# Layer 0's experts on one core: weight transfers are made to wait for the first slots, and six key projections go between the expert pairs

## The chip, the cores and the metric

The kernel runs on one core of one Trainium2 chip. The metric is the device time in microseconds. The kernel before was run three times: 2267.32, 2272.30 and 2272.84 us, a median of 2272.3 us. A separate execution was profiled; every row of a profile shown here is from that one execution. All times in rows are microseconds from the start of its span, unless a column says otherwise.

## What is computed

Four layers, each of them a cross attention followed by a mixture of experts, on 1024 tokens of width 256 (2 batches of 512) and a context of 2048 rows (2 batches of 1024). The change lies in layer 0's experts. Their reference, cut to what matters:

```python
logits = x @ router_w + router_b
route = softmax(logits, axis=1)
max_prob, max_ind = route.max(1), route.argmax(1)
for e in range(8):                       # experts, F = 1024
    h = x @ w1[e]                        # 256 -> 2048
    a, g = split(h, 2)
    y = silu(a) * g @ w2[e]              # 1024 -> 256
    out = where(max_ind == e, y, out)
out = out * max_prob
```

Layer 1's attention, which follows, needs keys and values of the normed context, `ctx @ Wkv`, for each of the two batches. They depend on nothing that layer 0's experts compute, so the kernel projects them early, during those experts.

## The kernel before

**Slots.** Each token's row is scattered to a place ("slot") in a DRAM buffer `xd`, sorted by expert, by eight indirect DMAs on GpSimd (L429; `si` holds the places). An expert has a front of 64 slots; what does not fit goes into overflow tiles of 128 slots, all of one expert. Slots come back as tiles `xs` of 128 rows, loaded by SyncE (L446). Each of these loads depends on all eight scatters.

**Tiles.** `pair_tile(s)` (four of them, s = 0 to 3) works on the fronts of experts 2s and 2s+1 at once: one `xs` tile, two weight tiles `w` loaded by SyncE at L465. `slot_tile(4 + s)` works on an overflow tile; its expert is known only at run time, so its weights are gathered by an indirect DMA on GpSimd (L524). Every weight tile has 3072 KB. The program order is pair 0, overflow tile 4, pair 1, tile 5, pair 2, tile 6, pair 3, tile 7, then tiles 8 and 9, and further tiles in a branch taken only if they are in use.

**Weight buffers.** The pool `L0g` has four buffers, handed out in turn: pair 0 takes buffers 0 and 1, tile 4 buffer 2, pair 1 buffers 3 and 0, tile 5 buffer 1, pair 2 buffers 2 and 3, tile 6 buffer 0, pair 3 buffers 1 and 2, and so on. Thus three of SyncE's transfers (both of pair 0, the first of pair 1) and tile 4's gather can start before any tile is computed; pair 1's second has to wait until pair 0 is done with buffer 0.

**Projections.** `ahead1(…, b)` makes the keys and values of layer 1 for batch `b` in 16 jobs: 8 of keys, then 8 of values. A job is two matmuls of 128x128 by 128x512 (four records in the trace, since each f32 matmul shows two) into a PSUM tile whose tag alternates between "a" and "g" (two buffers each, shared with the experts), a copy on ScalarE (L629 for keys, L649 for values) into `sk` (two buffers), and a 256 KB write to DRAM, issued by ScalarE (L633 to `kd`, L650 to `vd`). Batch 0 is done by `first_batch`, the `filler`, between the scatters and the first pair; batch 1 after the last tile. Then `combine` gathers the experts' results back, eight indirect DMAs on GpSimd (L609), and layer 1 starts with a layer norm of X.

**Order.** The order on each engine is set by the tile framework from the program order and its own priorities; each engine then runs its list strictly in order. A DMA signals its end on one of eight counters for SyncE and ScalarE together, handed out in turn, and a DMA that takes a counter again has a wait on it. GpSimd's DMAs have eight counters of their own.

Of the kernel before, what the change touches and what calls it, by code (L numbers as in the profile page):

```python
# [12 lines left out]
AF = mybir.ActivationFunctionType  # L13
# [4 lines left out]
P = 128  # L18
# [7 lines left out]
E = 8  # L26
# [7 lines left out]
def tile_kernel(ctx: ExitStack, tc: tile.TileContext, d: dict, out: bass.AP):  # L34
    nc = tc.nc
# [370 lines left out]

    FRONT = {"L0": E // 2, "L1": E, "L2": E, "L3": E}

    def moe(L, ps, hp, ep, rows, slots, wrow, used, F, act, glu, finish, filler=None, hold=None):

# [2 lines left out]
        front = FRONT[L]  # L415
        NS = front + wrow.shape[1]
        FT, W1 = F // P, (2 * F if glu else F)
        xd, yd = xds[L]
# [4 lines left out]
        for i, si in enumerate(slots):  # L423
            if named and i == 0:
                nc.vector.tensor_copy(rows[:, :, D], c_tok)
            for t in range(TT):
                if i == 1:
                    nc.vector.tensor_scalar(rows[:, t, D:], c_tok[:, t : t + 1], float(NT), None, ALU.add)
                x = nc.gpsimd.indirect_dma_start(  # L429
                    out=xd, out_offset=bass.IndirectOffsetOnAxis(ap=si[:, t : t + 1], axis=0), in_=rows[:, t, :], in_offset=None  # L430
                ).ins
# [5 lines left out]
        wd = d[f"{L}_experts"]  # L437
        WC = wd.shape[1]

        def parts(w):  # L440
            w1 = w[:, 0 : 2 * W1].rearrange("p (c f) -> p c f", c=2)
            return w1, w[:, 2 * W1 : 2 * W1 + FT * D].rearrange("p (t f) -> p t f", t=FT)

        def turned_slots(s):
            xs = hp.tile([P, RW], F32, tag="xs", name="xs", bufs=4)
            x = nc.sync.dma_start(xs, xd[s * P : (s + 1) * P, :]).ins  # L446
            for y in put:
                tc.add_manual_dep(
                    x, y.name, mybir.DependencyInfo(mybir.DependencyClass.Sync, mybir.DependencyReason.DATA),
                    reason="rows from any scatter",  # L450
                )
            pt = ps.tile([P, 2, P], F32, tag="mm", name="pt")
            for dc in range(2):
                nc.tensor.transpose(pt[:, dc, :], xs[:, dc * P : (dc + 1) * P], ident)
            sT = hp.tile([P, 2, P], F32, tag="sT", name="sT", bufs=3)
            nc.vector.tensor_copy(sT, pt)  # L456
            return xs, sT

        def pair_tile(s):


            ws = []
            for j in range(2):
                w = ep.tile([P, WC], F32, tag="w", name="w")
                nc.sync.dma_start(w, wd[(2 * s + j) * P : (2 * s + j + 1) * P, :])  # L465
                ws.append(parts(w))
            sT = turned_slots(s)[1]
            hT = hp.tile([P, FT, P], F32, tag="hT", name="hT")
            y = ps.tile([P, D], F32, tag="y", name="y")
            hs = {}  # L470

            def half(tag, c0):
                pa = ps.tile([P, 512], F32, tag=tag, name="p" + tag)
                for dc in range(2):
                    for j in range(2):
                        cols = slice(64 * j, 64 * j + 64)
                        nc.tensor.matmul(
                            pa[cols, :], sT[:, dc, cols], ws[j][0][:, dc, c0 : c0 + 512], start=(dc == 0), stop=(dc == 1)
                        )
                return pa  # L480

            def hidden(c, pa, pg):
                a = hp.tile([P, 512], F32, tag="act", name="act")
                nc.scalar.activation(a, pa, act)
                nc.vector.tensor_mul(a, a, pg)
                hs[c] = a

            def turn(c):
                pt = ps.tile([P, 4, P], F32, tag="mm", name="pt")
                for f in range(4):  # L490
                    nc.tensor.transpose(pt[:, f, :], hs[c][:, f * P : (f + 1) * P], ident)
                nc.vector.tensor_copy(hT[:, 4 * c : 4 * c + 4, :], pt)

            def product(c):
                for f in range(4 * c, 4 * c + 4):
                    for j in range(2):
                        cols = slice(64 * j, 64 * j + 64)
                        nc.tensor.matmul(
                            y[cols, :], hT[:, f, cols], ws[j][1][:, f, :], start=(f == 0), stop=(f == FT - 1)
                        )  # L500

            pa = half("a", 0)
            hidden(0, pa, half("g", F))
            pa = half("a", 512)
            turn(0)
            hidden(1, pa, half("g", F + 512))
            product(0)
            turn(1)
            product(1)
            yo = hp.tile([P, D], F32, tag="yo", name="yo", bufs=3)  # L510
            nc.scalar.copy(yo, y)
            nc.scalar.dma_start(yd[s * P : (s + 1) * P, :], yo)

        def slot_tile(s):
            w = ep.tile([P, WC], F32, tag="w", name="w")
            if s < front:
                x = nc.sync.dma_start(w, wd[s * P : (s + 1) * P, :]).ins
                if hold is not None and s < 4:
                    tc.add_manual_dep(
                        x, hold.name, mybir.DependencyInfo(mybir.DependencyClass.Sync, mybir.DependencyReason.DATA),  # L520
                        reason="not among the transfers that the attention waits for",
                    )
            else:
                nc.gpsimd.indirect_dma_start(  # L524
                    out=w, out_offset=None, in_=wd,
                    in_offset=bass.IndirectOffsetOnAxis(ap=wrow[:, s - front : s - front + 1], axis=0),
                )
            w1, w2 = parts(w)
            xs, sT = turned_slots(s)
            hT = hp.tile([P, FT, P], F32, tag="hT", name="hT")  # L530
            for f4 in range(0, FT, 4):
                pa = ps.tile([P, 4, P], F32, tag="a", name="pa")
                for f in range(4):
                    mm2(pa[:, f, :], w1, slice((f4 + f) * P, (f4 + f + 1) * P), sT, slice(0, P))
                to = hT[:, f4 : f4 + 4, :]
                if not glu:
                    nc.scalar.activation(to, pa, act)  # L537
                    continue
                pg = ps.tile([P, 4, P], F32, tag="g", name="pg")
                for f in range(4):  # L540
                    mm2(pg[:, f, :], w1, slice(F + (f4 + f) * P, F + (f4 + f + 1) * P), sT, slice(0, P))
                a = hp.tile([P, 4, P], F32, tag="act", name="act")
                nc.scalar.activation(a, pa, act)
                nc.vector.tensor_mul(to, a, pg)  # L544
            y = ps.tile([P, D], F32, tag="y", name="y")
            for f in range(FT):
                nc.tensor.matmul(y, hT[:, f, :], w2[:, f, :], start=(f == 0), stop=(f == FT - 1))  # L547
            yo = hp.tile([P, D], F32, tag="yo", name="yo", bufs=3)
            finish(yo, y, w)
            if not named:  # L550
                nc.scalar.dma_start(yd[s * P : (s + 1) * P, :], yo)
                return
            to = hp.tile([P, 2], F32, tag="to", name="to", bufs=8)
            nc.vector.tensor_scalar(to[:, 0:1], xs[:, D:], 2.0 * NT, float(s * P), ALU.is_ge, ALU.mult)
            nc.vector.tensor_add(to[:, 1:2], to[:, 0:1], xs[:, D:])
            ti = hp.tile([P, 1], I32, tag="ti", name="ti", bufs=8)
            nc.vector.tensor_copy(ti, to[:, 1:2])
            x = nc.gpsimd.indirect_dma_start(
                out=yd, out_offset=bass.IndirectOffsetOnAxis(ap=ti[:, 0:1], axis=0), in_=yo, in_offset=None
            ).ins  # L560
            for y in out_of:
                tc.declare_no_dep(x, y, reason="rows of different tokens")
            out_of.append(x)

        always = front + ALWAYS[L]
        if front == E:
            for s in range(always):
                slot_tile(s)
        else:
            for s in range(front):  # L570
                pair_tile(s)
                slot_tile(front + s)
            for s in range(2 * front, always):
                slot_tile(s)
# [61 lines left out]

    kds, vds = {}, {}

    def ahead1(ps, st, w, cT, b):

        if b == 0:
            kds["L1"] = dram.tile([B * 4 * P, S], F32, tag="L1kd", name="kd")
# [9 lines left out]
        jobs = []  # L652
# [1 line left out]
            for hf in range(2):  # L654
                jobs.append(("k", (b * 4 + pr) * P, hf * 512, slice(pr * P, (pr + 1) * P), b * S + hf * 512))
        jobs += [("v", kt) for kt in range(8)]
        ahead(ps, st, "L1", w, cT, jobs, values)

    def ahead16(ps, st, L, params, nkt):

# [95 lines left out]
    with (  # L756
# [39 lines left out]
        cT = cp.tile([P, 2, B * S], F32, tag="cT", name="cT")  # L796
        xn = kp.tile([P, TT, D], F32, tag="v", name="xn")
# [219 lines left out]
    with (  # L1017
# [23 lines left out]
            to_T(ps, cT, C, CT, g_c, b_c, "g")  # L1041
            ahead1(ps, hp, wkv, cT, 0)

        yd = moe("L0", ps, hp, ep, xn, slots, wrow, used, 1024, AF.Silu, True, plain, first_batch)
        ahead1(ps, hp, wkv, cT, 1)
        combine(fp.tile([P, TT, D], F32, tag="xn", name="yg"), yd, slots, [mp], X)


# [520 lines left out]
    first = {}  # L1569
# [268 lines left out]
```

## Time and profile before

| what | value |
|---|---|
| median of three runs | 2272.3 us |
| the profiled execution's own time | 2271.54 us |
| its span | 2269.7 us |
| TensorE busy | 2063.8 us, 91% of the span |
| VectorE, ScalarE, GpSimd busy | 1083.0, 859.2, 439.3 us |
| mean DMA rate over the span | 132 GB/s |
| layer 0's experts, first weight issue to first scores of layer 1 | 467.2 to 712.7 |

How to read a row of the timeline: start, duration, engine, line of the kernel, operation, output<-inputs, shape, count of records merged, and in brackets the idle time of the engine just before and what ended it. An engine with a "q" (SPq, ACTq) issues DMAs; the duration is that of issuing, not of the transfer. In a table by stage, each engine has its busy time and, in parentheses, its count of instructions; PEclk is the TensorE clock that was granted, 1.00 being full speed. The releaser in brackets is inferred: where a wait is for several things, the last by the profile is named.

### The profile page before, as it was taken

Reading aid. Unit: us, or ns where it says so; the run is one execution under the profiler, and the core shown is the slowest. Engines: PE = TensorE matmul, PEld = TensorE weight load, DVE = VectorE, ACT = ScalarE, POOL = GpSimd, SP = SyncE. Lnnn points to the kernel's source line nnn. Section 1 sums busy time; section 2 is a strip of 40 time slices with the busy share of each in tenths; the row PEclk is TensorE's granted clock in tenths of the full one; section 3 lists DMA queues with packets and bytes.
Section 4 is the critical chain, followed back from the end, with each engine's and each line's share of the span. In section 5 each row is a group of like instructions: output and inputs, shape, how many; then the busy total and the mean of one; then the engine's idle time right before and its main releaser. Section 6 shows DMA issues by size and latency. Waiting matters only on the chain. (4 is left out here: it accounts for less than half of the span.)

```text
span 2269.7 us, 29982 instructions
## 1 busy us (share of the span) xinstructions
PE 2063.8 (91%) x11532; PEld 1208.1 (53%) x11532; DVE 1083.0 (48%) x2157; ACT 859.2 (38%) x1645; POOL 439.3 (19%) x420
## 2 busy tenths in 40 slices
PE   7999999968898999999898898899699999579996
PEld 3444444444574445544686344589433333479995
DVE  7766666741124655665312884201377773422223
ACT  4444444421114656555112243222135556223333
POOL 2222223210012111210101122312123220111210
PEclk9999999988999999999899998999889999789998
DMA  4222222266835101000554612678410101547771
GB/s 128 70 61 75 70 74 58 88 266 268 332 126 130 47 28 38 28 10 28 179 179 157 230 40 74 219 284 312 138 47 28 32 19 25 249 180 294 312 310 64
DMA packets 111703, 300.72 MB, mean 132 GB/s; under 512 B 23232, under 2 KB 76224, under 8 KB 102848
## 3 DMA queue, kind: packets, MB, share of 16 engines
q1 hardware_dynamic: 76048, 159.30, 20.9%
q0 software_dynamic: 9888, 104.49, 11.9%
q10 hardware_dynamic: 25616, 34.90, 4.2%
q8 instruction: 97, 1.59, 0.3%
q14 instruction: 54, 0.44, 0.1%
HBM read 242.93 MB, written 47.66 MB: 128 GB/s over the span
## 5 line engine op out<-in xcount | busy, mean ns | idle before, releaser
L1432 ACT ACTIVATE p<-s 128x512 f32<-128x512 f32 (+3 forms) x384 | 185.9, 545 | 177.8 <-PE s L1431 116.3
L1374 PE MATMUL s<-kT,qT 32*128 32x512 f32 (+3 forms) x768 | 216.8, 603 | 8.7 <-DVE nm L1380 4.5
L132 PE MATMUL pa<-sT,w 128*128 128x128 f32 x1664 | 205.0, 278 | 8.7 <-DVE sT L456 3.7
L132 PEld LDWEIGHTS pa<-sT,w 128*128 128x128 f32 x1664 | 197.1, 193 | 17.2 <-ACT sq L1613 5.8
L547 PE MATMUL y<-w,hT 128*128 128x256 f32 x832 | 192.8, 384 | 9.3 <-ACT hT L537 4.3
L1431 PE MATMUL s<-qA,kT 32*128 32x512 f32 (+3 forms) x768 | 197.5, 592 | 1.3 <-ACT p L1432 0.9
L1384 DVE TENSOR_REDUCE mx<-s 128x1 f32<-128x512 f32 x256 | 163.5, 684 | 54.3 <-PE s L1374 33.6
L547 PEld LDWEIGHTS y<-w,hT 128*128 128x128 f32 x832 | 154.7, 192 | 31.7 <-DVE hT L544 6.1
L1119 ACT ACTIVATE p<-s,nm 128x512 f32<-128x512 f32 x192 | 129.3, 685 | 84.2 <-DVE nm L1116 84.2
L954 ACT ACTIVATE p<-s 128x1024 f32<-128x1024 f32 x128 | 124.1, 1021 | 90.0 <-PE s L949 90.0
L955 DVE TENSOR_SCALAR p<-p 128x1024 f32<-128x1024 f32 x128 | 108.4, 855 | 95.4 <-ACT p L954 95.4
L1116 DVE TENSOR_REDUCE nm<-s 128x2 f32<-128x1024 f32 x96 | 113.2, 1221 | 83.4 <-PE s L1112 83.4
L149 POOL TENSOR_TENSOR kT<-kT,turned 128x512 f32<-128x512 f32 x62 | 100.6, 1628 | 215.3 <-DVE turned L147 209.1
L960 DVE TENSOR_TENSOR acc<-acc,p 128x1024 f32<-128x1024 f32 x96 | 132.5, 1381 | 2.8
L132 PE MATMUL pg<-sT,w 128*128 128x128 f32 x1056 | 129.3, 276 | 0.0
L880 PE MATMUL o<-p,v 128*64 128x512 f32 x512 | 125.0, 606 | 3.8 <-DVE p L955 3.8
L949 PE MATMUL s<-qT,kT 64*128 64x512 f32 x512 | 127.2, 615 | 0.0
L544 DVE TENSOR_TENSOR hT<-act,pg 128x512 f32<-128x512 f32 x66 | 45.0, 687 | 169.7 <-PE pg L132 147.9
L132 PEld LDWEIGHTS pg<-sT,w 128*128 128x128 f32 x1056 | 123.9, 193 | 0.0
L148 POOL TENSOR_TENSOR kT<-kT,cos 128x512 f32<-128x512 f32 x62 | 87.8, 1425 | 134.7 <-DMA turned<-kT 63.4
L1407 PE MATMUL o<-p,v 128*32 128x256 f32 (+3 forms) x1280 | 107.3, 406 | 6.9 <-POOL p L1436 6.7
L1133 PEld LDWEIGHTS pt<-ident,p 128*128 128x128 f32 x768 | 86.4, 142 | 49.7 <-issue 24.5
(295 smaller groups left out, 3039.6 us busy)
## 6 DMA issues: line engine op xcount, KB each, us to landing
w<-in_L_experts_dram SPq DMA_DIRECT2D x8, 3200.0 KB
w<-in_L_experts_dram SPq DMA_DIRECT2D x8, 3072.0 KB
w<-in_L_experts_dram SPq DMA_DIRECT2D x8, 2048.0 KB
w<-in_L_experts_dram SPq DMA_DIRECT2D x8, 1536.0 KB
kd<-sk ACTq DMA_DIRECT2D x40, 256.0 KB
kT<-kd SPq DMA_DIRECT2D x16, 512.0 KB
turned<-kT SPq DMA_DIRECT2D x60, 128.0 KB
v<-vd SPq DMA_DIRECT2D x12, 512.0 KB
```

Source lines behind the costliest of these rows:

```text
L132: nc.tensor.matmul(ps_ap, lhsT[:, dc, lcols], rhs[:, dc, rcols], start=(dc == 0), stop=(dc == 1))
L547: nc.tensor.matmul(y, hT[:, f, :], w2[:, f, :], start=(f == 0), stop=(f == FT - 1))
L880: nc.tensor.matmul(G[n]["o"][64 * j : 64 * j + 64, :], V[g, b][:, kt, pr * P + 64 * j : pr * P + 64 * j + 64], p[:, j, :], start=(kt == 0) ...
L949: nc.tensor.matmul(s1[:, j, :], G[n]["kT"][r, kt * P : (kt + 1) * P], G[n]["qT"][r, :], start=True, stop=True)
L954: G[n]["exp"] = nc.scalar.activation(p, s1, AF.Exp, scale=0.125).ins
L960: nc.vector.tensor_add(G[n]["acc"], G[n]["acc"], p)
L1116: nc.vector.tensor_reduce(nm[:, qt, :, c], s1, AX.X, ALU.max, negate=True)
L1119: nc.scalar.activation(p[:, j, :], s1[:, j, :], AF.Exp, bias=nm[:, qt, j, c : c + 1], accum_out=l[:, qt, j, c : c + 1],)
L1374: nc.tensor.matmul(s1[:, :w], qT[r, qt * P : (qt + 1) * P], kT[r, c * 512 : c * 512 + w], start=True, stop=True)
L1384: nc.vector.tensor_reduce(mx[:, qt, j, c : c + 1], s1, AX.X, ALU.max)
L1431: nc.tensor.matmul(s2[:, qs], kT[r, kt * P : (kt + 1) * P], qA[r, qs], start=True, stop=True)
L1432: nc.scalar.activation(p[:, j, qs], s2[:, qs], AF.Exp, scale=0.25)
```

## The change

It has two parts. First, weight transfers get a dependence on the first `xs` load, so that they are issued only when it has landed: those of pairs 1 to 3 (of which only the first of pair 1 started earlier before) and the gather of overflow tile 4. Second, `ahead1` gets a slice of its job list, and `moe` a hook between the pairs: before pairs 1, 2 and 3 two key jobs each of batch 1 are run, and the other ten jobs stay behind the last tile.

```diff
+        first_slots = []
+        def behind_slots(x):
+            tc.add_manual_dep(x, first_slots[0].name, ...Sync...)
...
         def turned_slots(s):
             x = nc.sync.dma_start(xs, xd[s * P : (s + 1) * P, :]).ins
+            first_slots.append(x)
...
         def pair_tile(s):
-                nc.sync.dma_start(w, wd[(2 * s + j) * P : (2 * s + j + 1) * P, :])
+                x = nc.sync.dma_start(w, wd[(2 * s + j) * P : (2 * s + j + 1) * P, :]).ins
+                if s > 0:
+                    behind_slots(x)
...
         def slot_tile(s):
-                nc.gpsimd.indirect_dma_start(out=w, ...)
+                x = nc.gpsimd.indirect_dma_start(out=w, ...).ins
+                if front < E and s == front:
+                    behind_slots(x)
...
             for s in range(front):
+                between(s)
                 pair_tile(s)
                 slot_tile(front + s)
...
-        ahead(ps, st, "L1", w, cT, jobs, values)
+        ahead(ps, st, "L1", w, cT, jobs[part], values)
...
+        def between(s):
+            if s > 0:
+                ahead1(ps, hp, wkv, cT, 1, slice(2 * s - 2, 2 * s))
...
-        yd = moe("L0", ps, hp, ep, xn, slots, wrow, used, 1024, AF.Silu, True, plain, first_batch)
-        ahead1(ps, hp, wkv, cT, 1)
+        yd = moe("L0", ps, hp, ep, xn, slots, wrow, used, 1024, AF.Silu, True, plain, first_batch, None, between)
+        ahead1(ps, hp, wkv, cT, 1, slice(6, None))
```

As the changed program is built, GpSimd's list has the eight scatters ahead of tile 4's gather, where before the gather stood first. SyncE's list has pair 0's two weights, the context transfer `cTr` (2048 KB, for layer 2), four `xs` loads, and then the first weights of pair 1, which stood third before. ScalarE's and TensorE's lists have the six key jobs between an overflow tile and the next pair; VectorE's list is unchanged. The waits change with the order: the eighth value write of batch 0 (L650) takes the counter of pair 1's first weights and waits for them, and the first `xs` load waits on a counter last used by batch 0's first key write instead of by its seventh.

More of the change, by code (lines that the diff above doesn't have):

```diff
@@ L407, in tile_kernel, with moe @@
     FRONT = {"L0": E // 2, "L1": E, "L2": E, "L3": E}
-    def moe(L, ps, hp, ep, rows, slots, wrow, used, F, act, glu, finish, filler=None, hold=None):
+    def moe(L, ps, hp, ep, rows, slots, wrow, used, F, act, glu, finish, filler=None, hold=None, between=None):
         front = FRONT[L]
@@ L438, in moe @@
         WC = wd.shape[1]
+        first_slots = []
+        def behind_slots(x):
+            tc.add_manual_dep(
+                x, first_slots[0].name, mybir.DependencyInfo(mybir.DependencyClass.Sync, mybir.DependencyReason.DATA),
+                reason="not among the transfers that the first tile waits for",
+            )
         def parts(w):
@@ L523, in slot_tile @@
             else:
-                nc.gpsimd.indirect_dma_start(
+                x = nc.gpsimd.indirect_dma_start(
                     out=w, out_offset=None, in_=wd,
                     in_offset=bass.IndirectOffsetOnAxis(ap=wrow[:, s - front : s - front + 1], axis=0),
-                )
+                ).ins
+                if front < E and s == front:
+                    behind_slots(x)
             w1, w2 = parts(w)
@@ L637, in tile_kernel, with ahead1 @@
     kds, vds = {}, {}
-    def ahead1(ps, st, w, cT, b):
+    def ahead1(ps, st, w, cT, b, part=slice(None)):
         if b == 0:
```

## The prediction

> **What bounds the kernel now.** The page has TensorE busy for 91% of the span, so I looked for places where TensorE stands idle or slow inside the stretch that the change touches (467 to 713 us). The table by stage of that stretch comes first:
>
> ```profile
> 499.00:502.00 3.00, 0.15 (x1) 0.00 (x0) 0.00 (x0) 0.00 (x0) 2.17 (x3) 1.00 0.97 367
> 502.00:505.00 3.00, 0.00 (x0) 0.00 (x0) 0.00 (x0) 0.00 (x0) 0.74 (x1) 0.74 0.87 301
> ...
> 535.00:540.00 5.00, 4.20 (x30) 1.99 (x28) 2.07 (x3) 1.09 (x2) 0.00 (x0) 1.00 0.00 0
> ...
> 556.00:560.00 4.00, 0.68 (x4) 0.22 (x4) 0.00 (x0) 0.00 (x0) 0.00 (x0) 0.76 0.95 404
> 560.00:564.00 4.00, 4.00 (x10) 1.03 (x10) 0.00 (x0) 0.50 (x1) 0.00 (x0) 0.50 1.00 429
> ```
>
> Where TensorE (first column) is idle, the DMA share (last but one) is near 1; at 535 to 540 no byte moves. After an idle stretch the granted clock is 0.50. The timeline says what is moved and who waits:
>
> ```profile
> 467.20 1.28 SPq L465 DMA_DIRECT2D w<-in_L_experts_dram  x3
> 492.59 1.20 POOL L524 DMA_INDIRECT w<-in_L_experts_dram,wrow  x1 [38.40 <-DMA kd<-sk]
> 494.10 1.00 POOL L429 DMA_INDIRECT xd<-xn,si  x1 [0.30 <-issue]
> 506.97 0.97 POOL L429 DMA_INDIRECT xd<-xn,si  x1 [4.23 <-DMA w<-in_L_experts_dram,wrow]
> 507.54 0.58 ACT L629 COPY sk<-pk 128x512 f32<-128x512 f32 x1 [11.10 <-DMA kd<-sk]
> 508.18 6.42 PE L132 MATMUL pk<-wkv,cT 128*128 128x512 f32 x8 [9.02 <-ACT sk L629]
> 517.05 12.26 PE L132 MATMUL pk<-wkv,cT 128*128 128x512 f32 x24 [2.46 <-ACT sk L629]
> 559.79 2.82 PE L477 MATMUL pa<-w,sT 128*64 128x512 f32 x5 [3.33 <-DMA w<-in_L_experts_dram]
> 590.44 1.50 PE L477 MATMUL pa<-w,sT 128*64 128x512 f32 x5 [2.65 <-DMA w<-in_L_experts_dram]
> 618.70 2.07 PE L477 MATMUL pa<-w,sT 128*64 128x512 f32 x5 [2.78 <-SPq L575]
> ```
>
> Four weight tiles are in flight from 467 to 507. Beside them a 256 KB key write takes 10 to 12 us, `sk` has two buffers, so ScalarE's copies wait, then TensorE's projections of batch 0 (9.0 and 2.5 us). The first pair stands behind those projections. Tile 4's gather also goes ahead of all scatters on GpSimd, and the eighth scatter waits for it. Later, each of pairs 1 to 3 waits for its second weight tile. Two more views end the stretch: SyncE's waits from 460 to 560, and the timeline at its end:
>
> ```profile
> SPq L446 <- DMA kd<-sk: 10.8, 2, 10.6
> ...
> 684.00 0.21 ACT L62 ACTIVATE rsq<-rsq 128x8 f32<-128x8 f32 x1 [4.91 <-DVE rsq L61]
> ...
> 698.68 3.28 DVE L98 TENSOR_SCALAR xn<-X,mv,rsq 128x256 f32<-128x256 f32 x8 [12.96 <-PE pk L132]
> ```
>
> The first slot load (issued at 520.62) ended its wait on a key write, which has nothing to do with slots: it had taken that write's completion counter. And layer 1's norm, ready at 685.7, waits for batch 1's last projection at 698.6.
>
> **Part 1: the slots go first.** Scatters: `si` is written by 491.67. Layer 1's experts have this order already: there `si` is written at 1113.50, the first scatter starts at 1113.78 and the slot load is issued at 1125.50, 11.7 us on. So here: scatter at 491.95, slot load at 503.7, landed at 505.6 (1.9 us, a load of layer 3 in the chain of waits), not 522.5. Its counter is now the first key write's, long done.
>
> Pair 0's two tiles alone end the weight traffic near 483 (6.3 MB at the 425 GB/s of 470 to 490). `cTr`, freed by the transposes of C, then follows at about 485 and not 507.5. So the key copies run at TensorE's pace: 24 records took 10.7 us where nothing stopped them, 1.75 us a job, and uncongested copies came two in 3.7 us (520.6 to 531). I put the eighth key copy at 500, value copies at 502, 503, 505.5, 506.6, 508.7.
>
> Then the two waiting transfers start, near 506. Two such tiles issued together took 15.9, 15.2 and 15.4 us before (543.9 to 559.8, 575.2 to 590.4, 603.3 to 618.7), some 400 GB/s; with 1.3 MB of value writes between them I take 17 us: landed at 523. What is caught with them is the fourth and later value writes, at 10 to 12 us each as above: sixth copy at 520, seventh at 522, eighth at 524.2.
>
> [...] The row at 507.54 shows ScalarE held 11.1 us for a write. The eighth value write is bound to pair 1's first weights by the counter, and in ScalarE's list the table load (1.28 us) and pair 0's first silu stand behind it; behind the silu stand VectorE's product, TensorE's transposes and all the rest of pair 0. [...] Before, the silu started at 534.9. **Gain 8.4**, less 0.6 for a cold clock after TensorE's new wait (bounds: none, and the 2.4 us that 5 us of half speed cost at 560): pair 0 ends at 536.0, not 543.8. **Gain 7.8**, bounds 0 and 18.
>
> Tile 4's weights (landed 523) are needed only at 536. The new wait of the gather holds nothing on GpSimd but later gathers; on SyncE the weights stand behind four slot loads whose counters are done, and before them no load is delayed.
>
> **Part 2: six jobs into the gaps.** Two jobs are 3.5 us of TensorE, two copies and two write issues on ScalarE (2 x 0.58 + 2 x 0.33 = 1.8 us, while it has no silu to do), and 0.5 MB of writes. A period from pair end to pair end lasted 31.4, 28.1 and 29.9 us, 89.4 in sum. Its work is an overflow tile of 10.5 us (543.8 to 554.3) and a pair of 15.0 us (528.7 to 543.8), so 25.5; the rest is waiting and cold clock. With the jobs it is 29.0 by TensorE. By DMA: second weights issued at the pair's end, landed 15.4 later, 12.8 us of work after that (590.4 to 603.2) is 28.2. TensorE decides: 3 x 29.0 = 87.1, a **gain of 2.3**. [...] The rows differ: gaps of 3.3 and 2.8 us were followed by matmuls of over 1.0 us for 4 to 5 us, one of 2.65 was not. [...] Contention from the writes: they are issued some 14 us into a load of 15.4, so I cost 0.2, bounds 0 and 1.3 us a period (0.5 MB at 400 GB/s). **Gain 2.1**.
>
> **The tail.** After the last tile (668.0) ten jobs remain. Their copies run to the fifth at 677, then ScalarE waits with the layer norm's square root for VectorE (684.0), which hangs on the gathers and doesn't move: 16.0 us after the branch, as before. Five more copies then took 7.9 us (684.0 to 691.9), so the last value write is issued near 24 us after the branch, not 32.7. The key fetch of layer 1, issued at 701.86 right after the last writes, follows it. Gain 8.1 by this, 11.4 if TensorE's six jobs of 1.9 us (30.6 for 16) counted in full; I take **9.0**, nearer the queue. The norm no longer waits: its projection ends at about 687 before shifts, its own input at 685.7.
>
> Sum: 7.8 + 2.1 + 9.0 = 18.9 from the profiled execution's own 2271.5 us, so 2252.6; the median of the runs is 0.8 above that execution. Forecast **2253**, own range 2245 to 2260. Nothing behind layer 1's start is touched.
>
> **Rivals.** (a) *The front gain is lost*: waiting weights land near 533 rather than 523, the silu is back where it was; 2271.5 - 2.1 - 9 = 2260. For it: the counter. Against it: two tiles in 15 to 16 us, three times. 0.14.
> [...] 0.14.
> (c) *The jobs move but hide nothing*: each gap stays beside its 3.5 us (10.5 lost), front gain 6, tail 9: 2267. For it: the DMA share is 0.95 to 1.00 in the gaps. 0.10.
> (d) *Slower: loads pace the pairs.* Without the early loads, pair 1's and tile 4's transfers, the value writes and then the key writes come bunched, and the rate falls to the 300 GB/s of 502 to 505. Then the first two land at 531, front gain 1, and later second weights take 22.7 us (6.3 + 0.5 MB): 3 x (22.7 + 12.8) = 106.5, 17 lost; 2271.5 + 17.1 - 1 - 9 = 2279. It decides from a load time of 20.5 us on, against 15.2 to 15.9 measured. 0.10.
> The forecast has 0.52.
>
> **The numbers.** No change that a measurement of this kernel can tell is within 0.3%, 6.8 us. Faster: forecast, (a), (b), 0.80. Same: (c), 0.10. Slower: (d), 0.10. The range of 8 in 10 reaches from (b) to just past (a): 2242 to 2264.
>
> **What would show it.** First slot load issued at about 504; tile 4's gather behind the scatters; no wait of TensorE at 499; a write issue of ScalarE at L650 (changed line number) that ends with pair 1's weights, at 521 to 526, and the silu right behind. Pair ends at 536, 565, 594, 623. No 1.0 us matmuls in pairs 1 to 3. Branch at 658, ten copies, square root at 674, first scores of layer 1 near 694. Wrong if the eighth write is issued long before the weights land, if the second weights of a pair take over 20 us, or if the gaps ahead of pairs keep 3 us beside the jobs.

## The result, and the profile after

| kernel | median | runs | lowest to highest | ratio to before, 95% interval |
|---|---|---|---|---|
| before | 2270.9 us | 13 | 2263.8 to 2280.4 | |
| changed | 2259.5 us | 13 | 2253.1 to 2265.2 | 0.9954 [0.9937, 0.9971] |

The change makes the kernel faster by 11.4 us of the medians. The forecast was 18.9 us, so the time lies inside the range, near its upper end, and where rival (a) put it (2260). The profiled execution of the changed kernel took 2264.7 us, with a span of 2262.7 us. The timeline of the changed kernel shows what became of the front:

```profile
468.34 0.80 SPq L475 DMA_DIRECT2D w<-in_L_experts_dram  x2
473.96 6.93 PE L132 MATMUL pl<-rw,xT 128*128 128x8 f32 x32
495.98 1.22 POOL L429 DMA_INDIRECT xd<-xn,si  x1 [43.41 <-DVE si L379]
502.79 13.90 PE L132 MATMUL pk<-wkv,cT 128*128 128x512 f32 x32
508.61 1.84 SPq L455 DMA_DIRECT2D xs<-xd  x4
511.09 0.33 SPq L475 DMA_DIRECT2D w<-in_L_experts_dram  x1
511.09 0.36 ACTq L665 DMA_DIRECT2D vd<-sv  x1
511.98 0.98 POOL L536 DMA_INDIRECT w<-in_L_experts_dram,wrow  x1 [5.92 <-DMA vd<-sv]
512.36 0.33 ACTq L665 DMA_DIRECT2D vd<-sv  x1
...
528.40 0.59 ACT L664 COPY sv<-pk 128x512 f32<-128x512 f32 x1 [16.07 <-DMA vd<-sv]
529.03 3.68 PE L489 MATMUL pa<-w,sT 128*64 128x512 f32 x8 [12.13 <-ACT sv L664]
532.09 0.59 ACT L664 COPY sv<-pk 128x512 f32<-128x512 f32 x1 [3.11 <-DMA vd<-sv]
...
535.40 0.33 ACTq L665 DMA_DIRECT2D vd<-sv  x1
537.11 1.09 ACT L496 ACTIVATE act<-pa 128x512 f32<-128x512 f32 x2
```

The order is the one that was meant: pair 0's weights, scatters, slots, then the two waiting transfers. The waits of 9.0 and 2.5 us in TensorE's projections are gone (the row at 502.79 is one block of 32 records). But a wait of 12.1 us has come up at 529.03, ahead of pair 0's own matmuls. It ends with a value copy, and that copy waited 16.1 us for a value write. The first silu starts at 537.1; before, it started at 534.9.

SyncE's waits from 460 to 560, in the changed kernel, answer to the row that named a key write before (columns: total, times, longest):

```profile
SPq L455 <- DMA xd<-xn,si: 19.2, 3, 18.1
```

The slot load now waits for the scatters, which it needs, and for no key write. The table by stage of the changed kernel (TensorE's busy time first; clock, DMA share and GB/s last):

```profile
516.00:520.00 4.00, 0.91 (x4) 0.28 (x2) 0.42 (x1) 0.00 (x0) 0.00 (x0) 1.00 1.04 443
520.00:524.00 4.00, 0.00 (x0) 0.00 (x0) 0.00 (x0) 0.00 (x0) 0.00 (x0) 0.61 1.00 429
524.00:528.00 4.00, 0.00 (x0) 0.00 (x0) 0.00 (x0) 0.00 (x0) 0.00 (x0) 0.50 1.04 423
528.00:532.00 4.00, 2.96 (x8) 0.77 (x8) 0.00 (x0) 0.59 (x1) 0.00 (x0) 0.50 0.42 161
...
556.00:561.00 5.00, 4.50 (x14) 2.19 (x13) 0.42 (x1) 1.54 (x3) 0.00 (x0) 1.00 1.02 437
561.00:565.00 4.00, 3.94 (x18) 1.29 (x20) 0.00 (x0) 0.60 (x1) 0.00 (x0) 1.00 1.02 437
```

From 520 to 528 no engine is busy at all while the DMA engines run full (share 1.00 and 1.04): everything waits for the waiting transfers to pass. After 528 the rate falls (161 GB/s from 528 to 532); the trace's list of transfers gives the gather 19.1 us from issue to landing, so the last of the two tiles is in near 531. The last two rows are the gap ahead of pair 1, which was idle before and is full now. The same timeline, for pair 1 and for the end of the stretch:

```profile
556.68 3.60 PE L132 MATMUL pk<-cT,wkv 128*128 128x512 f32 x8
561.06 2.34 PE L489 MATMUL pa<-w,sT 128*64 128x512 f32 x7 [0.56 <-ACT sk L644]
...
682.75 0.21 ACT L62 ACTIVATE rsq<-rsq 128x8 f32<-128x8 f32 x1 [4.84 <-DVE rsq L61]
686.88 3.28 DVE L98 TENSOR_SCALAR xn<-X,mv,rsq 128x256 f32<-128x256 f32 x8 [2.40 <-PE pk L132]
700.95 1.99 PE L1132 MATMUL s<-kT,qT 64*128 64x512 f32 x8 [1.74 <-POOL kT L149]
```

Two key jobs stand in the gap, and the wait behind them is 0.6 us where it was 3.3. At the end the norm waits 2.4 us for TensorE, not 13.0.

| part (us of the profiled executions) | before | after | gained | forecast |
|---|---|---|---|---|
| end of pair 0 | 543.8 | 546.0 | -2.2 | 7.8 |
| three periods, pair 0's end to pair 3's end | 89.4 | 85.0 | 4.4 | 2.1 |
| pair 3's end to the branch | 34.8 | 35.1 | -0.2 | 0 |
| branch to the first scores of layer 1 | 44.7 | 34.9 | 9.7 | 9.0 |

These sum to 11.7 us at the first scores of layer 1. The span is only 7.0 us shorter: 4.7 us are lost later in that execution, in stages that the change leaves alone; over the whole execution the mean granted clock was 0.950 against 0.958. The medians give 11.4.

So the second part of the change did what was expected, and more. The question is the first part: why did it gain nothing? Three causes were on the table when the experiments were planned. **A**: value writes of batch 0 are caught beside the two waiting tiles, for longer than I had put. **B**: the counter that the eighth value write shares with pair 1's weights holds ScalarE, as the prediction had it. **C**: the front was only unlucky in its clock. The router's matmuls (`pl`, x32) took 6.9 us in this execution, at a granted clock of 0.50 (473.9 to 480.9), and 3.9 us before, at 0.93 (472.7 to 476.7), and everything behind them is late.

### The profile page after: what moved, and what is told of

It is laid out like the page before. It is cut to its first block, busy times and chain, and to the rows that moved or that the text cites. A ratio compares the mean times of both kernels' runs of the same rounds, so it can differ in the third digit from the quotient of the medians.

```text
span 2262.7 us, 29983 instructions
## 1 busy us (share of the span) xinstructions
PE 2070.5 (92%) x11532; PEld 1218.9 (54%) x11532; DVE 1083.6 (48%) x2157; ACT 859.6 (38%) x1645; POOL 439.3 (19%) x420
```

## The experiments

The kernel before ran again beside each group: 2270.3 us in 19 runs beside the first four, 2273.2 us in 12 runs beside the last four. The ratios are to these, and each edit is shown against the changed kernel.

### Each part of the change alone

The first part alone: the hook between the pairs does nothing, and batch 1's 16 jobs all stay behind the last tile.

```diff
         def between(s):
-            if s > 0:
-                ahead1(ps, hp, wkv, cT, 1, slice(2 * s - 2, 2 * s))
+            return
...
-        ahead1(ps, hp, wkv, cT, 1, slice(6, None))
+        ahead1(ps, hp, wkv, cT, 1)
```

> The first part alone: the waiting weights, with all 16 jobs of batch 1 behind the last tile. Theory A (the value writes of batch 0 are caught beside the two weight tiles that wait, and ScalarE's copies with them): pair 0 ends 76 to 78 us after the first weight issue, as in both profiles (76.6 before, 77.6 changed), pairs 1 to 3 still wait for their second weights, ratio to before 0.998 to 1.003. Theory B (the prediction's sizes, ScalarE held by the eighth value write's counter until pair 1's weights land): pair 0 ends 69 us after the first weight issue and ScalarE's issue of the eighth write ends with those weights, ratio 0.996 to 0.997. Theory C (the front gain is there, and a cold TensorE clock in the router hid it in the one changed profile): pair 0 ends 73 to 74 us after, ratio 0.997 to 0.998.

Measured: 2273.1 us in 14 runs, ratio 1.0006 [0.9992, 1.002]. The second part alone: no transfer waits for the slots.

```diff
         def behind_slots(x):
+            return
```

> The second part alone: the six jobs between the pairs, weights and gather as before. All theories: the three periods sum to 85 to 88 us (89.4 before), the tail is 9 to 10 us shorter. Theory A: with the first part worth nothing, this is all of the change: ratio 0.993 to 0.995, within 3 us of the changed kernel. Theories B and C: the first part adds 4 to 8 us, so this one is slower than the changed kernel by that: ratio 0.997 to 0.9985 by the prediction's sizes.

Measured: 2257.5 us in 6 runs, ratio 0.9945 [0.9925, 0.9965]. The change as a whole has 0.9954 [0.9937, 0.9971]. The second part is all of the gain; the first is worth nothing that can be measured. In the first part's profile pair 0 ends 77.6 us after the first weight issue (76.6 before), as A had it. In the second part's profile the three periods sum to 85.8 us, and the way from the branch to the first scores takes 35.0 us. The timeline of the first part alone has the gaps ahead of the pairs back:

```profile
561.85 2.78 PE L489 MATMUL pa<-w,sT 128*64 128x512 f32 x5 [3.07 <-DMA w<-in_L_experts_dram]
...
591.50 1.73 PE L489 MATMUL pa<-w,sT 128*64 128x512 f32 x5 [2.47 <-DMA w<-in_L_experts_dram]
...
621.61 1.50 PE L489 MATMUL pa<-w,sT 128*64 128x512 f32 x5 [2.93 <-SPq L590]
```

That of the second part alone has one short wait left in their place:

```profile
559.86 1.50 PE L490 MATMUL pa<-w,sT 128*64 128x512 f32 x5 [0.86 <-DMA w<-in_L_experts_dram]
```

So the gaps are closed by the jobs, with or without the waits on the slots.

### The value writes taken out of the way

If A holds, the loss in front goes when no value write meets a waiting tile. There are two ways to get there. In the first, both tiles wait for the last value write of batch 0 rather than for the slots:

```diff
         def behind_slots(x):
             tc.add_manual_dep(
-                x, first_slots[0].name, ...
+                x, value_writes[7].name, ...
...
+    value_writes = []
...
-            nc.scalar.dma_start(vds["L1"][r, :], v)
+            value_writes.append(nc.scalar.dma_start(vds["L1"][r, :], v).ins)
```

> The changed kernel, but the waiting transfers (tile 4's gather, pair 1's first weights) depend on the last value write of batch 0 instead of on the first slots. Theory A: with no weights beside them the value copies run two in 3.7 us, the first silu comes 52 to 56 us after the first weight issue (68.8 in the changed kernel, 67.7 before), pair 0 ends at 62 to 66 us; tile 4 then waits for its weights until about 72, so 4 to 6 us of it remain: 2252 to 2256 us. Theory B: the same front, since the counter is released by the dependence itself, but no gain beyond 3 us. Theory C: no change in the front against the changed kernel.

Measured: 2250.1 us in 6 runs, ratio 0.9903 [0.9879, 0.9928]; by the ratios that is 0.5%, some 11 us, below the changed kernel. In the other, four of batch 0's eight value jobs go behind the last tile, and the waits stay as in the change:

```diff
...
-            ahead1(ps, hp, wkv, cT, 0)
+            ahead1(ps, hp, wkv, cT, 0, slice(0, 12))
...
         ahead1(ps, hp, wkv, cT, 1, slice(6, None))
+        ahead1(ps, hp, wkv, cT, 0, slice(12, None))
```

> The changed kernel, but only the first 4 of batch 0's 8 value jobs stay ahead of pair 0, and the other 4 go behind the last tile. Theory A: no value copy is left to be caught, pair 0 starts as soon as the slots are in, its first silu comes 48 to 52 us after the first weight issue and pair 0 ends near 60; the four jobs cost 7 us in the tail; in sum 2248 to 2253 us. Theory B: nothing stands behind a counter of weights any more, the same. Theory C: the front gains nothing, and the tail's 7 us make it slower than the changed kernel: 2264 to 2268.

Measured: 2247.9 us in 6 runs, ratio 0.9899 [0.9875, 0.9922]. The timeline of the kernel whose tiles wait for the last value write:

```profile
516.94 0.59 ACT L665 COPY sv<-pk 128x512 f32<-128x512 f32 x1 [0.46 <-DMA vd<-sv]
...
520.30 0.60 ACT L496 ACTIVATE act<-pa 128x512 f32<-128x512 f32 x1
...
538.07 3.75 PE L132 MATMUL pa<-sT,w 128*128 128x128 f32 x16 [7.84 <-DMA w<-in_L_experts_dram,wrow]
```

The eighth value copy is at 516.9 (it was at 534.8), the silu at 520.3 (537.1), and pair 0 ends at 529.9 (546.0). Half of that is given back at once: tile 4 now waits 7.8 us for its weights. With four values late pair 0 ends at 519.7, and tile 4 waits 6.0 us:

```profile
510.06 0.60 ACT L496 ACTIVATE act<-pa 128x512 f32<-128x512 f32 x1
...
525.67 3.76 PE L132 MATMUL pa<-sT,w 128*128 128x128 f32 x16 [6.04 <-DMA w<-in_L_experts_dram,wrow]
```

Some 7 us of that front are the four jobs themselves, which are only moved: that kernel takes 42.0 us from the branch to the first scores of layer 1, where the changed kernel takes 34.9. The kernel with the waits on the last value write moves no job, so it is the cleaner of the two.

The kernel whose tiles wait for the last value write had the slow router too (7.0 us), and its pair 0 ended 16 us earlier all the same. So C alone can't be the cause of the loss; its share is told below.

### How long a write is caught: one tile beside it

A and B are told apart by letting pair 1's weights start only after the last value write, while tile 4's gather still follows the slots. The counter can then hold nothing.

```diff
-        def behind_slots(x):
+        def behind_slots(x, y=None):
             tc.add_manual_dep(
-                x, first_slots[0].name, ...
+                x, (y or first_slots[0]).name, ...
...
-                    behind_slots(x)
+                    behind_slots(x, value_writes[7])
```

> Of the two waiting transfers, only tile 4's gather still starts with the first slots; pair 1's first weights wait for the last value write of batch 0. So one weight tile is in flight beside the value writes, not two. Theory A (value writes are caught beside the waiting tiles, and how long depends on how much is in flight beside them): a value write takes about 10 us beside one tile against 17 to 20 beside two, and the gather alone is done after 8 to 10 us, so only the third and fourth copy are late; first silu of pair 0 at 522 to 528, between 520.3 (nothing beside) and 537.1 (both); pair 0 ends at 532 to 537; time 2251 to 2257. Theory B (the counter of pair 1's weights holds ScalarE): pair 1's weights start only after the last value write and cannot hold it, so all of the gain is had: silu at 520 or before, time about 2250. If the delay is the same beside one tile as beside two: silu at 537, time 2259.

Measured: 2251.0 us in 4 runs, ratio 0.9917 [0.9886, 0.9948]. Its timeline:

```profile
512.03 0.98 POOL L536 DMA_INDIRECT w<-in_L_experts_dram,wrow  x1 [6.11 <-DMA xs<-xd]
512.24 0.33 ACTq L666 DMA_DIRECT2D vd<-sv  x1
...
523.14 0.58 ACT L665 COPY sv<-pk 128x512 f32<-128x512 f32 x1 [7.90 <-DMA vd<-sv]
...
525.01 0.59 ACT L665 COPY sv<-pk 128x512 f32<-128x512 f32 x1 [1.28 <-DMA vd<-sv]
...
528.37 0.60 ACT L496 ACTIVATE act<-pa 128x512 f32<-128x512 f32 x1
528.67 0.33 SPq L475 DMA_DIRECT2D w<-in_L_experts_dram  x1
...
537.24 2.05 PE L132 MATMUL pa<-sT,w 128*128 128x128 f32 x16
```

The write issued at 512.24, just behind the gather, frees its buffer at 523.1, after 10.9 us; the silu is at 528.4, between 520.3 and 537.1. Pair 1's weights are issued at 528.67, behind the silu's start, so no counter of theirs can have held it. B is out, and the delay grows with what is in flight. Tile 4 follows pair 0 at 537.24 without a wait, which makes up for the other kernel's earlier silu: there tile 4 waited 7.8 us.

### Pair 1's first weights early, as before

Tile 4's wait in the kernels above suggests issuing pair 1's first weights with pair 0's again, so that the gather has the queues to itself. Three kernels have this edit (shown in part): with the gather behind the slots, behind the last value write, and with four values late.

```diff
+        first_ws = []
+        if front < E:
+            first_ws = [ep.tile([P, WC], F32, tag="w", name="w") for _ in range(4)]
+            for i in range(3):
+                nc.sync.dma_start(first_ws[i if i < 2 else 3], wd[i * P : (i + 1) * P, :])
...
         if filler is not None:
             filler()
...
-                w = ep.tile([P, WC], F32, tag="w", name="w")
-                x = nc.sync.dma_start(w, wd[(2 * s + j) * P : (2 * s + j + 1) * P, :]).ins
-                if s > 0:
-                    behind_slots(x)
+                i = 2 * s + j
+                if i < 3:
+                    w = first_ws[i if i < 2 else 3]
+                else:
+                    w = ep.tile([P, WC], F32, tag="w", name="w")
+                    nc.sync.dma_start(w, wd[i * P : (i + 1) * P, :])
...
-            w = ep.tile([P, WC], F32, tag="w", name="w")
+            w = first_ws[2] if front < E and s == front else ep.tile([P, WC], F32, tag="w", name="w")
```

In these three the context transfer `cTr` (2.1 MB) stands behind the slot loads in SyncE's list and is issued at 503.7 to 505.0.

> The changed kernel, but pair 1's first weights are issued together with pair 0's two at about 467, as in the kernel before; only tile 4's gather waits for the first slots. The context transfer of 2 MB now stands behind the four slot loads in SyncE's list. Theory A: early, a third tile delays some key writes by little (the third tile ends near 490, while the key writes are still few); late, the value writes meet one tile and the context transfer, 5 MB rather than 6 MB, so the value copies are still late: silu at 528 to 537, time 2253 to 2260. Against it, if the early tile slows the key writes as much as four early tiles did before, TensorE waits for a key copy by 5 us or more ahead of the slots, and the time is 2262 or more.

Measured: 2255.2 us in 7 runs, ratio 0.9936 [0.9915, 0.9958]. Its timeline:

```profile
523.31 0.59 ACT L671 COPY sv<-pk 128x512 f32<-128x512 f32 x1 [14.30 <-DMA vd<-sv]
```

The silu is at 529.4. The context transfer has taken the place of the tile that was moved away, and the value writes are caught again.

> Pair 1's first weights early as in the run before, and tile 4's gather behind the last value write. Theory A: value writes meet only the context transfer; copies run freely, silu at 520 to 524, pair 0 ends at 530 to 534; the gather alone takes 8 to 10 us from about 520 and has landed when pair 0 ends, so the wait of 7.8 us ahead of tile 4, seen where both tiles waited for the last value write, is gone: time 2241 to 2246. If the early third tile costs what it saves there: 2250. If the context transfer catches the value writes as a weight tile does: silu at 528 or later, 2253 or more.

Measured: 2251.2 us in 6 runs (2247.8 to 2263.0), ratio 0.9926 [0.9898, 0.9954]. Its timeline:

```profile
513.11 0.58 ACT L672 COPY sv<-pk 128x512 f32<-128x512 f32 x1 [6.40 <-DMA vd<-sv]
...
521.07 1.08 ACT L503 ACTIVATE act<-pa 128x512 f32<-128x512 f32 x2
...
533.72 2.90 PE L132 MATMUL pa<-sT,w 128*128 128x128 f32 x16 [3.34 <-DMA w<-in_L_experts_dram,wrow]
```

The marks in the front are where they were expected (silu 521.1, pair 0's end 530), and tile 4's wait is 3.3 us, shorter but not gone. The time, expected at 2241 to 2246, is 5 us above that and no better than with both tiles behind the value writes. The profiled execution, at 2247.8 us, was the fastest of the six, so its trace can't tell where the others lost time. This stays open.

> Four value jobs of batch 0 go behind the last tile, pair 1's first weights are issued early, the gather waits for the first slots. With the four values late and both tiles waiting, pair 0 ended at 519.7 and tile 4 then waited 6.0 us for its gather. If that wait was the gather sharing the queues with pair 1's weights, it goes: time 2240 to 2244. If the early third tile takes the time back at the key writes, 2247 to 2252; TensorE would then wait for a key copy in front of the slots.

Measured: 2243.8 us in 5 runs, ratio 0.9888 [0.986, 0.9915], the fastest kernel here, by the ratios some 15 us below the changed kernel. Its interval overlaps that of the kernel with four values late and no early weights, so the early weights' own share isn't shown. In the profiles it reaches the first scores of layer 1 2.1 us ahead of that kernel (686.2 against 688.4), and 1.8 us of this lead were there at the first weight issue (465.0 against 466.8). Its timeline:

```profile
510.16 1.08 ACT L503 ACTIVATE act<-pa 128x512 f32<-128x512 f32 x2
...
522.47 3.75 PE L132 MATMUL pa<-sT,w 128*128 128x128 f32 x16 [3.37 <-DMA w<-in_L_experts_dram,wrow]
```

### The writes side by side

A value copy needs the buffer of the copy two before it, so the time from a write's issue to that later copy bounds how long the write took from above. Where the copy waited for the write, it is the write's time. The big transfers in flight are named with their sizes:

| kernel | big transfers beside the write | MB | write issued to buffer reused, us |
|---|---|---|---|
| both tiles behind the last value write | none | 0 | 2.1 to 3.4 |
| before (key write of 508.15) | `cTr` | 2.1 | 8.3 |
| early pair 1, gather behind values | `cTr` | 2.1 | 8.0, 9.3 |
| one tile beside | gather | 3.1 | 10.9, 9.8 |
| before (key writes of 495.43 and 496.47) | gather | 3.1 | 12.1, 12.7 |
| early pair 1 | gather, `cTr` | 5.2 | 16.8, 15.3 |
| changed kernel | gather, pair 1's first | 6.3 | 17.3, 19.7 |

At the 400 GB/s that the pairs' tiles had, 2.1, 3.1, 5.2 and 6.3 MB are 5.2, 7.9, 13.1 and 15.7 us. Each write took that and 2 to 5 us more. In this kernel, then, a 256 KB write issued beside big transfers ended about when they did, and did not get ahead of them. That is a description of these rows; what inside the DMA engines makes it so was not tested.

## Why the prediction was right and wrong

**The sum: inside the range, in part by luck.** The front brought 10.0 us less than forecast, and the other parts 2.8 us more. The kernel before also ran a little faster in the comparison (2270.9 us) than the 2272.3 us from which the forecast started. From 2272.3, a gain of 11.4 us would have been 2260.9, just outside the range.

**The direction, and the second part: right.** The jobs fill the gaps, the clock stays at 1.00 ahead of pair 1 (rows of 556 to 565), and the second weights are never late again. Periods were mis-sized on the careful side: 28.7, 27.9 and 28.4 us, not 29.0 each. A gain of 2.1 was forecast and 4.4 came. The term that was off is the pair, 15.0 us by the first pair before: it takes 13.6 us as pair 1 (561.06 to 574.69) and 12.8 as pair 2. The overflow tile was right (10.7 for 10.5), and the two jobs cost more than their 3.5 us, 4.4 from the tile's end to the pair's start (556.68 to 561.06).

**The tail: right in size and in mechanism.** The square root came 16.7 us after the branch (16.0 forecast), the last value write 23.5 us after it (24 forecast), and the gain was 9.7 us for 9.0. The norm still waited 2.4 us for TensorE, where the prediction had next to none.

**The front: wrong.** Forecast were a silu at 526.5 (the 534.9 of before, less the gain of 8.4) and 7.8 us gained; it came at 537.1, and the first part alone measures 1.0006. The gain of 8.4 had ScalarE held at the eighth write's issue until pair 1's weights land, a term that no run shows; in its place the runs showed copies that came late ahead of that write (16.1 us of waiting at 528.40), and a late start. Two terms failed.

The term that failed on its own account is "What is caught with them is the fourth and later value writes, at 10 to 12 us each as above". The 10 to 12 us were read from key writes before, which I had placed beside four weight tiles. Two of the three such writes stood beside one: three tiles issued at 467 are through near 490 at the 425 GB/s that the prediction uses, and these writes were issued at 495 and 496, beside the gather alone. The table by stage and the timeline of the kernel before show it:

```profile
487.00:490.00 3.00, 3.00 (x19) 2.26 (x19) 1.29 (x9) 0.45 (x1) 0.00 (x0) 1.00 0.98 404
490.00:493.00 3.00, 3.00 (x8) 1.33 (x7) 1.68 (x13) 0.14 (x1) 0.41 (x1) 1.00 0.72 278
493.00:496.00 3.00, 3.00 (x8) 1.07 (x7) 0.00 (x0) 0.73 (x2) 2.40 (x3) 1.00 0.63 156
```

```profile
495.43 0.33 ACTq L633 DMA_DIRECT2D kd<-sk  x1
...
496.47 0.33 ACTq L633 DMA_DIRECT2D kd<-sk  x1
...
509.15 0.58 ACT L629 COPY sk<-pk 128x512 f32<-128x512 f32 x1 [1.03 <-DMA kd<-sk]
```

(The third, issued at 484.56, took 10.2 us beside what was left of the three tiles, by the same rate some 2 to 3 MB.) Beside the two tiles that the change lets loose together, a write takes 17 to 20 us. Also, the third write is caught, not only the fourth. It goes out in the same moment as pair 1's weights, at 511.09, though its copy was done at 510.50. So its issue seems to have waited for the slots too; the trace doesn't name what it waited for. The tiles' own time was put too short as well: 6.3 MB and the 1.3 MB of value writes are 19 us at the 400 GB/s that the prediction names, not 17, and the gather took 19.1. From the slot load's issue to the silu the prediction had 22.8 us (503.7 to 526.5). The trace has 28.5 (508.61 to 537.11), so this step cost 5.7 of the 10.6 us.

The other 4.9 us are the start: the slot load was issued at 508.6, not 503.7. Pair 0's weights were issued 1.1 us later than before, and the router's 32 matmuls took 6.9 us instead of 3.9; from the first scatter to the slot load it took 12.6 us for 11.7. I had taken the router as unchanged. It was slow (over 6 us) in the profiled executions of four kernels and fast (3.9 to 4.6 us) in the other six. All four slow ones let pair 1's first weights wait, but so does one of the fast ones, and no edit touches what runs ahead of the router. Whether it belongs to a build or to an execution is not settled. It can't have taken all of the gain: the kernels with both tiles, or with pair 1's weights alone, behind the last value write had the slow router too, and those executions took 2253.0 and 2251.7 us against 2264.7.

**The counter: a step that didn't bind.** That ScalarE would stand at the issue of the eighth write was not shown: here that write had nothing to wait for. It was issued at 535.40, some 4 us after the last weights had landed, because the copies ahead of it were late. (The row at 507.54 is a copy that waits for its buffer, not a write that waits to be issued. What the kernel before does show ahead of an issue is SyncE's wait of 10.6 us on a key write, ahead of the slot load.) The run with one tile beside the writes shows the silu held to 528.4 with no such counter in play. Rival (a) named the counter for its case, so it has the right time, but not by the cause that it named.

**Rivals.** (b), the front's upper bound of 18 us gained, was not had by the change, but by taking the value writes out of the way: a silu at 520.3 or 510.1. Its price was too high for all that, since tile 4 then waits for its gather (6.0 to 7.8 us). (c) is refuted by the wait of 0.6 us at 561.06, and (d) by periods of 28 us; loads do not pace the pairs.

**The marks.** Pair ends were put at 536, 565, 594 and 623 and came at 546.0, 574.7, 602.6 and 631.0; the branch at 658 came at 666.0, the first scores at 694 at 701.0. The distances between them hold within about a microsecond, and the front's 10 us run through all of them, shrinking to 7.

## What to carry to other kernels

When transfers are held back so that a first tile gets its data sooner, look at what small writes are issued in the moment they are let go. Here the stall only moved, from key writes ahead of the slots to value writes behind them, and moving four of those writes, or holding the tiles back until they were out, gave what the change was after. When a transfer's time is taken from a row, add up the bytes in flight in the moment of its issue, in that row and in the changed kernel; a congested row is a price for that load and for no other (here 8.0 to 19.7 us for the same 256 KB beside 2.1 to 6.3 MB).

## What the hardware showed unexpectedly

A 256 KB write took 2.1 to 3.4 us with no big transfer beside it and 17 to 20 us beside 6.3 MB, about as long as the big transfers themselves. And identical matmuls of the router took 3.9 us in one kernel's execution and 6.9 us in another's: after the same waits of 1.69 and 0.79 us, at 455.93 and 457.80 before and at 454.31 and 456.17 after, the granted clock of 460 to 468 was 1.00 in the first and 0.79 in the second. Before these waits the changed kernel was 1.6 us ahead of the kernel before (the table load of L62 starts at 451.90, against 453.52); at the router's end it was 4 us behind.
